# A state-space scan whose decay factors move from SBUF to PSUM, with one 128-channel block and two states per step

## Chip, cores and metric

The kernel runs on one core of one Trainium2 chip. The metric is the device time of one execution in microseconds (us). The kernel before takes 4627.35 us (median of three runs, 4623.8 to 4629.94).

## What is computed

The reference runs one layer of a hybrid model on an input of 8 batches, each of 512 tokens and 256 channels: an attention part with 16 heads, a feed-forward net (FFN) whose operands are quantised to a four-bit format, a two-way Mamba block, and the same FFN again. The change touches the Mamba block. Cut to what matters, it does this once per direction:

```python
x_dbl = xc @ xproj_w                                   # xc: [batch, token, 512 channels]
dt, B_ssm, C_ssm = split(x_dbl, [64, 64 + 16])         # 16 states
dt = softplus(dt @ dt_w + dt_b)
dA = exp(dt[..., None] * A)                            # [.., channel, state]
dBu = dt[..., None] * B_ssm[:, :, None, :] * xc[..., None]
h = dA_t * h + dBu_t                                   # over the tokens
y_t = sum over states of h * C_t
y = y + xc * D_skip
```

There are 8 batches x 2 directions x 512 channels x 16 states of such recurrences, each 512 tokens long.

## The kernel before, in words

The work is written as Python generators. `thread_a` is attention of a batch, `thread_b` the FFNs, the merge and the front of Mamba (`mamba_pre`), and `thread_s` the scan (`ssm`) with its preparation (`ssm_prep`). `interleave` takes rounds of them in turn. A scheduler that knows the dependences then orders each engine's instructions, once, when the kernel is built. On the chip each engine runs its own list strictly in that order, so an instruction that waits also holds everything behind it on its engine. DMAs are issued by SyncE (SP), which has such a list too.

The scan (`ssm`, L818) holds 128 channels on the partitions and 512 tokens along the free dimension. A step handles **two blocks of 128 channels in one state**. There are 8 x 2 x 2 x 16 = 512 steps, each with these instructions:

- L825: SP loads the B row and the C row of the state, repeated on all 128 partitions (tile `rep`, 512 KB, four buffers). Its source `bcd` is a scratch tensor in memory.
- L829: ScalarE computes two exponentials 128x512 into `abuf` in SBUF, the decay factors. There is one such buffer (`NA = 1`).
- L830: VectorE multiplies `u` (step size times input) by B into `hbuf`, 128x1024. There are three `hbuf` buffers.
- L834: VectorE runs one `tensor_tensor_scan` over both blocks, 128x1026. A zero column between the blocks stops the recurrence. Direction 1 runs over reversed views.
- L835: GpSimd multiplies `hbuf` by C in place, 128x1024. The text below calls it the step's product with C.
- L838: TensorE adds the eight 128x128 pieces into PSUM by transposing matmuls. One bank per block sums all 16 states (`y0`, `y1`).

After 16 steps ScalarE copies the sums out (L844), TensorE transposes them back (L127), VectorE adds `xc * D_skip` (L852), and SP writes the result (L853).

The eight PSUM banks are shared out by name: `pa` 2 and `po` 1 for attention, `pb` 2 for FFN and merge, `pp` 1 for Mamba's front, the scan's preparation and its transposes back, `y0` and `y1` for the sums.

Other lines that the prediction names: L384, L438 and L443 (attention, VectorE reading PSUM), L573 and L574 (FFN, VectorE reading PSUM and SBUF), L755 (merge, VectorE reading PSUM and SBUF), L500 to L510 (quantisation: VectorE, with GpSimd at L506 and L510), L693 and L695 (convolution of Mamba's front, VectorE with two SBUF inputs), L270 to L275 (reciprocal square root, tiny VectorE instructions), L811 to L816 (preparation of the scan, GpSimd and VectorE), L469 (attention, ScalarE's exponentials from PSUM to SBUF).

Of the kernel before, what the change touches and what calls it, by code (L numbers as in the profile page):

```python
# [18 lines left out]
P = 128  # L19
# [16 lines left out]
def shape_constants():  # L36
    """Tables and masks that depend on shapes alone, side by side in one array."""
    inv = (1.0 / (np.float32(10000.0) ** (np.arange(0, LAT, 2, dtype=np.float32) / np.float32(LAT)))).astype(np.float32)
    fr = np.outer(np.arange(T, dtype=np.float32), inv).astype(np.float32)
    cos = np.repeat(np.cos(fr), 2, axis=-1).astype(np.float32)  # L40
    sin = np.repeat(np.sin(fr), 2, axis=-1).astype(np.float32)
    cos = np.tile(cos.T, (4, 1))
    sin = np.tile(sin.T, (4, 1))
    p = np.arange(P)
    mask8 = (p[:, None] // HD == np.arange(8)[None, :]).astype(np.float32)
    mask4 = (p[:, None] // LAT == np.arange(4)[None, :]).astype(np.float32)
    up = np.where(p[None, :] > p[:, None], NEG, 0.0).astype(np.float32)
# [15 lines left out]
def tile_hybrid(ctx: ExitStack, tc: tile.TileContext, w: dict, consts: bass.AP, out: bass.AP):  # L63
# [11 lines left out]
    PB, TB, HB, QB, QA, HT = 2, 3, 3, 3, 2, 1  # L75
    LAG, TC, XB, YT = 2, 4, 3, 2
    NH4, NA, NU, NDT, TA, RB = 3, 1, 3, 2, 2, 4
# [8 lines left out]
    BANKS = {"pa": 2, "po": 1, "pb": 2, "pp": 1, "y0": 1, "y1": 1}  # L86
# [13 lines left out]
    # ---------------------------------------------------------------- constants  # L100
# [52 lines left out]
    def prep_attention():  # L153
# [6 lines left out]
        q2r = work([P, LAT], F32, "qmx", 4)  # L160
        k2r = work([P, LAT], F32, "qns", 4)
        l2r = work([LAT, HD], F32, "l2r", 1)
        wqr = work([P, LAT], F32, "qrs", 4)
# [11 lines left out]
        k2n = work([LAT, HD], F32, "k2n", 1)  # L175
# [66 lines left out]
        # cproj, transposed, and the vector that every bias behind the softmax adds up to  # L242
# [65 lines left out]
    def token_transpose(dst, src, tag="pb"):  # L308
        """src [P, NT, C] tokens on partitions -> dst [P, 2, T] channels on partitions."""
# [64 lines left out]
    def roped(xT, g, q):  # L374
        """Rotated latents of four heads [latent, token]; q: 0 for queries, 1 for keys."""
# [13 lines left out]
    def spill(hl, order):  # L389
        """hl [(head, latent), high/low, token] -> memory [part, latent, head, token] with the parts in order."""  # L390
# [6 lines left out]
    def latents(xT, g):  # L397
        """High and low parts of the keys and of the queries of four heads, in memory."""
# [27 lines left out]
            # row maxima, negated  # L426
# [62 lines left out]
    # -------------------------------------------------------------------- FFN  # L489
    def fp4(dst, src, n, tag, twice=False, pp=P):  # L490
        """Block-wise FP4 quantise and dequantise of src [pp, n] along the free dim into dst. A multiple of the step
        (half of the power of two below the value, at least 0.5) is what is left when 1.5 * 2**23 steps have been added
        and taken away again; or-ing 22 << 23 into an exponent of 128 or 129 adds 22 to it, and leaves a smaller one
        below 149."""
        nb = n // 16
        mx = work([P, FF // 16], F32, "qmx", 4)[:pp, :nb]
        s3 = src.rearrange("p (b k) -> p b k", k=16)
        V.tensor_reduce(mx, s3, AX.X, ALU.max, apply_absolute_value=True)
        ns = work([P, FF // 16], F32, "qns", 4)[:pp, :nb]
        V.tensor_scalar(ns, mx, -1.0 / 6.0, -2e-12 if twice else -1e-12, ALU.mult, ALU.min)  # L500
        rs = work([P, FF // 16], F32, "qrs", 4)[:pp, :nb]
# [46 lines left out]
    def ffn_front(src):  # L548
        """The normalised and quantised rows, transposed."""
# [52 lines left out]
    def ffns(jobs):  # L602
        """One FFN after the other, as one stream of row tiles; the rows of the next are made ready meanwhile."""
# [26 lines left out]
    # ------------------------------------------------------------------ Mamba  # L630
# [9 lines left out]
    abuf = [const([P, 2, T + 1], F32, f"abuf{i}") for i in range(NA)]  # L640
    hbuf = [const([P, 2, T + 1], F32, f"hbuf{i}") for i in range(NH4)]
    for t in abuf + hbuf:
        G.memset(t, 0.0)
# [53 lines left out]
    def mamba_pre(src, scr):  # L697
# [13 lines left out]
        token_transpose(xT, xn, "pp")  # L711
        yield
        for m in range(8):
            wp = work([P, 2, P], F32, "xrf", XB)
            nc.sync.dma_start(wp, win_d[m])
            o = psum("pp")
# [56 lines left out]
    def ssm_prep(b, d, c, scr):  # L773
        """Step sizes of half the channels in one direction and their products with the input; B and C in memory."""
        sx = ("", "_b")[d]
        if c == 0:
# [6 lines left out]
            o = psum("pp")  # L783
# [17 lines left out]
        for e in range(2):  # L801
            o = psum("pp")
# [15 lines left out]

    def ssm(b, d, scr):
        for c in range(2):  # L820
            dt, u, bcd = prep.pop((b, d, c))
            yps = [psum(f"y{i}") for i in range(2)]
            for n in range(NS):
                bcr = work([P, 2, T], F32, "rep", RB)
                nc.sync.dma_start(bcr, bcd[n][None].to_broadcast([P, 2, T]))  # L825
                seq[0] += 1
                a, h = abuf[seq[0] % NA], hbuf[seq[0] % NH4]
                for m in range(2):
                    S.activation(a[:, m, 1:], dt[:, m, :], AF.Exp, scale=Aneg[:, d, 2 * c + m, n : n + 1])  # L829
                V.tensor_tensor(h[:, :, 1:], u, bcr[:, 0, None, :].to_broadcast([P, 2, T]), ALU.mult)  # L830
                aflat, hflat = a.rearrange("p m t -> p (m t)"), h.rearrange("p m t -> p (m t)")
                if d == 1:
                    aflat, hflat = aflat[:, ::-1], hflat[:, ::-1]
                V.tensor_tensor_scan(hflat, aflat, hflat, 0.0, ALU.mult, ALU.add)  # L834
                G.tensor_tensor(h[:, :, 1:], h[:, :, 1:], bcr[:, 1, None, :].to_broadcast([P, 2, T]), ALU.mult)  # L835
                for m in range(2):
                    for i in range(NT):
                        PE.matmul(yps[m][:, i * P : (i + 1) * P], h[:, m, 1 + i * P : 1 + (i + 1) * P], ident,  # L838
                                  start=(n == 0 and i == 0), stop=(n == NS - 1 and i == NT - 1), is_transpose=True)
                yield  # L840
            yts = []
            for i in range(2):
                yts.append(work([P, T], F32, "yt", YT))
                S.copy(yts[i], yps[i])  # L844
            for i in range(2):
                o = psum("pp")
                for q in range(NT):
                    transpose(o[:, q * P : (q + 1) * P], yts[i][:, q * P : (q + 1) * P])
                xp = work([P, T], F32, "xp", 1)
                m = 2 * c + i  # L850
                nc.sync.dma_start(xp, scr["xc"][4 * d + m])
                V.scalar_tensor_tensor(xp, xp, Dh[:, d, m : m + 1], o, ALU.mult, ALU.add)  # L852
                nc.sync.dma_start(scr["y"][4 * d + m], xp)  # L853
# [13 lines left out]
    def both(*gens):  # L867
        """The generators in turns until every one has ended."""
# [10 lines left out]
    def thread_b(done, pre, new):  # L879
        """Merge and second FFN of batch done, Mamba's front of batch pre, first FFN of batch new."""  # L880
# [4 lines left out]
    def interleave(*gens):  # L885
        """Rounds of the generators, each stretched over the same number of rounds and ahead of its place by a number
        of instructions."""
# [43 lines left out]
    seq = [0]  # L931
# [56 lines left out]
```

## Time and profile before

| what | value |
|---|---|
| median of three runs | 4627.35 us |
| span of the profiled execution | 4625.4 us |
| busy VectorE (DVE) | 4028.7 us |
| busy TensorE (PE) | 3244.4 us |
| busy GpSimd (POOL) | 2201.7 us |
| busy ScalarE (ACT) | 1592.1 us |
| memory moved | 628.44 MB, mean 136 GB/s |
| of it loads of `rep` | 512 of 512 KB |
| first and last scan start | 541.1 and 4502.8 us |

A profile is one execution. Its page gives busy times per engine, the span cut in 40 slices, and the costliest groups of instructions. A group's line names the source line, the engine, the operation, output and inputs with shapes, the count, the busy time and the mean duration in ns of one, and after the last bar how long the engine sat idle before these instructions and on what. Views of the trace add to this: one line's instructions with their shortest, median and longest duration, all instructions of an engine in order of time, busy times per stretch, and who waited for whom. A duration runs from an instruction's start on its engine to its end, so time in which it stands still inside the engine counts as busy.

### The profile page before, as it was taken

To read this page: it belongs to the slowest core of one execution; us is meant where nothing else is said; L and a number is where in the kernel's file an instruction comes from. 1 tells how busy PE (TensorE), PEld (TensorE's weight loads), DVE (VectorE), ACT (ScalarE), POOL (GpSimd) and SP (SyncE) were. 2 spreads that over 40 slices of the span, in tenths; PEclk is the share of its full clock that TensorE was granted. 3 is DMA by queue.
4 is the path that set the end of the run, shared out by engine and by line. 5 is a ranking of instruction groups with operands and counts; after the bars stand their busy time and mean duration, and the time that the engine had idled before them with its cause. 6 is when DMAs were issued, how large, how long until landed. Compare 5 with 4: busy or idle time off the path is not lost. (4 is left out here: it accounts for less than half of the span.)

```text
span 4625.4 us, 40263 instructions
## 1 busy us (share of the span) xinstructions
PE 3244.4 (70%) x12904; PEld 2000.0 (43%) x12904; DVE 4028.7 (87%) x4087; ACT 1592.1 (34%) x2725; POOL 2201.7 (48%) x929
## 2 busy tenths in 40 slices
PE   4879777787776678777777777768745566466456
PEld 2334344344444345444544444445533344345344
DVE  5235599897999996999989998999999999999983
ACT  1223432543443333333343333433433324332320
POOL 3011365445445653545444564565455554555551
PEclk8779878888887799888888888878866777677678
DMA  5223433444454344543454344533543244425232
GB/s 138 85 82 103 141 133 115 152 145 147 159 188 138 115 130 156 166 148 121 153 180 156 119 139 159 185 114 119 167 140 125 100 130 162 147 100 189 98 103 88
DMA packets 349922, 628.44 MB, mean 136 GB/s; under 512 B 50029, under 2 KB 195726, under 8 KB 349710
## 3 DMA queue, kind: packets, MB, share of 16 engines
q1 hardware_dynamic: 349710, 625.85, 41.9%
q8 instruction: 103, 1.69, 0.2%
q14 instruction: 109, 0.89, 0.1%
HBM read 506.85 MB, written 118.88 MB: 135 GB/s over the span
## 5 line engine op out<-in xcount | busy, mean ns | idle before, releaser
L835 POOL TENSOR_TENSOR hbuf<-hbuf,rep 128x1024 f32<-128x1024 f32 x512 | 1304.8, 2549 | 1505.4 <-DVE hbuf L834 688.3
L834 DVE TENSOR_TENSOR_SCAN hbuf<-abuf,hbuf 128x1026 f32<-128x1026 f32 x512 | 1357.7, 2652 | 32.8 <-ACT abuf L829 30.7
L829 ACT ACTIVATE abuf<-dt,Aneg 128x512 f32<-128x512 f32 x1024 | 684.9, 716 | 1699.9 <-DVE hbuf L834 1688.0
L830 DVE TENSOR_TENSOR hbuf<-u,rep 128x1024 f32<-128x1024 f32 x512 | 911.6, 1786 | 37.0 <-issue 19.6
L838 PE MATMUL y<-cst,hbuf 128*128 128x128 f32 x4096 | 690.5, 322 | 355.2 <-POOL hbuf L835 346.7
L838 PEld LDWEIGHTS y<-cst,hbuf 128*128 128x128 f32 x4096 | 579.1, 169 | 517.8 <-POOL hbuf L835 422.9
L98 PE MATMUL pb<-wgu,fxT 128*128 128x352 f32 x1024 | 427.9, 555 | 167.8 <-DVE hff L573 55.5
L433 PE MATMUL pa<-kst,qst 96*128 96x512 f32 (+3 forms) x512 | 229.9, 497 | 237.3 <-DVE tmp L384 100.9
L474 PE MATMUL po<-pt,vs 128*32 128x512 f32 (+3 forms) x1024 | 343.5, 481 | 4.3 <-ACT pt L469 4.2
L98 PEld LDWEIGHTS pb<-wgu,fxT 128*128 128x128 f32 x1024 | 211.5, 223 | 311.3 <-DVE hff L573 75.8
L98 PE MATMUL pa<-xT,wp 128*128 128x512 f32 x512 | 288.1, 694 | 50.4 <-DVE mx L443 29.3
L386 POOL TENSOR_TENSOR tmp<-tmp,tmp 128x512 f32<-128x512 f32 x64 | 124.4, 1944 | 405.8 <-DVE tmp L384 247.6
L98 PE MATMUL pb<-qv,hff 128*128 128x256 f32 x1024 | 261.4, 402 | 38.5 <-DMA qv<-sy 36.0
L98 PE MATMUL pb<-wdn,hT 128*128 128x256 f32 (+1 forms) x768 | 238.9, 455 | 34.5 <-ACT hT L588 14.6
L469 ACT ACTIVATE pt<-pa 128x512 f32<-128x512 f32 x320 | 186.0, 591 | 197.4 <-PE pa L466 135.5
L433 PEld LDWEIGHTS pa<-kst,qst 96*128 96x128 f32 x512 | 120.0, 235 | 305.3 <-DVE tmp L384 123.6
L443 DVE TENSOR_REDUCE mx<-pa 128x1 f32<-128x512 f32 (+2 forms) x384 | 179.0, 497 | 82.7 <-PE pa L435 82.4
L693 DVE SCALAR_TENSOR_TENSOR tmpB<-xs,cw,tmpB 128x512 f32<-128x512 f32 x192 | 243.0, 1265 | 7.6 <-ACT tmpB L691 6.1
L464 PE MATMUL pa<-qst,kst 98*128 98x512 f32 (+3 forms) x512 | 213.5, 464 | 50.4 <-ACT pt L469 23.3
L98 PEld LDWEIGHTS pb<-qv,hff 128*128 128x128 f32 x1024 | 197.3, 201 | 86.0 <-DMA hff<-in_merge_w 22.9
L98 PEld LDWEIGHTS pb<-wdn,hT 128*128 128x128 f32 (+1 forms) x768 | 161.1, 225 | 93.2 <-issue 25.8
L510 POOL TENSOR_TENSOR hff<-qv,qns 128x704 f32<-128x704 f32 x66 | 143.7, 2177 | 104.7 <-DVE qv L509 79.0
(207 smaller groups left out, 4899.3 us busy)
## 6 DMA issues: line engine op xcount, KB each, us to landing
rep<-bcd SPq DMA_DIRECT2D x512, 512.0 KB
hld<-hl SPq DMA_DIRECT2D x192, 256.0 KB
hff<-in_merge_w SPq DMA_DIRECT2D x128, 256.0 KB
qv<-sy SPq DMA_DIRECT2D x128, 256.0 KB
kst<-hld SPq DMA_DIRECT2D x64, 384.0 KB
qst<-hld SPq DMA_DIRECT2D x64, 384.0 KB
wp<-wqk_d SPq DMA_DIRECT2D x64, 256.0 KB
sxc<-tmpB SPq DMA_DIRECT2D x64, 256.0 KB
```

The costliest lines, as they stand in the source:

```text
L98: PE.matmul(o, L, R, start=start, stop=stop, **kw)
L433: PE.matmul(o[:, at : at + n], qst[pr][:96, j, i * P : (i + 1) * P], kst[:96, j, :n], start=(k == 0), stop=False)
L443: V.tensor_reduce(M[:, j, i : i + 1], o[:, at : at + n], AX.X, ALU.max, negate=True)
L464: PE.matmul(o[:, at : at + n], kst[:, j, kt * P : (kt + 1) * P], qst[pr][:, j, kt * P :], start=(k == 0), stop=False)
L469: S.activation(pt, o, AF.Exp)
L474: PE.matmul(po[c : c + 32, kt * P :], vs[:, kt, h * VW : h * VW + 32], pt[:, at : at + n], start=(kt == 0), stop=(kt == 2), tile_position= ...
L693: V.scalar_tensor_tensor(acc, tap(k), cw[:, d, m, k : k + 1], acc, ALU.mult, ALU.add)
L829: S.activation(a[:, m, 1:], dt[:, m, :], AF.Exp, scale=Aneg[:, d, 2 * c + m, n : n + 1])
L830: V.tensor_tensor(h[:, :, 1:], u, bcr[:, 0, None, :].to_broadcast([P, 2, T]), ALU.mult)
L834: V.tensor_tensor_scan(hflat, aflat, hflat, 0.0, ALU.mult, ALU.add)
L835: G.tensor_tensor(h[:, :, 1:], h[:, :, 1:], bcr[:, 1, None, :].to_broadcast([P, 2, T]), ALU.mult)
L838: PE.matmul(yps[m][:, i * P : (i + 1) * P], h[:, m, 1 + i * P : 1 + (i + 1) * P], ident, start=(n == 0 and i == 0), stop=(n == NS - 1 and ...
```

## The change

A step now handles **one block of 128 channels in two states**. There are again 512 steps.

- The decay factors go to PSUM: two banks `a`, one exponential 128x512 each, instead of `abuf` in SBUF. The zero column is gone.
- The scan becomes two instructions of 128x512 per step, each with its factors in PSUM and its `h` in SBUF. `h` has four buffers.
- The B and C rows of two states are loaded together: 1 MB per step instead of 512 KB, and three buffers instead of four. A row that served two blocks is now loaded for each block.
- ScalarE issues these loads, and those of `xp`, instead of SP. Each is queued behind the second exponential of a step, and fetches for two steps later.
- A block's sums take one bank `y`, and are finished after 8 steps; L844 to L853 of before run once per block.
- The banks `pp`, `y0`, `y1` become `a` (2) and `y` (1). What used `pp` now uses `pb`.
- To make room in SBUF the buffers of `qv`, `tmpB`, `yt` and the three small quantisation tiles go down by one each.

The diff, cut to this (some lines with names of pools and tags are left out):

```diff
-    PB, TB, HB, QB, QA, HT = 2, 3, 3, 3, 2, 1
-    LAG, TC, XB, YT = 2, 4, 3, 2
-    NH4, NA, NU, NDT, TA, RB = 3, 1, 3, 2, 2, 4
+    PB, TB, HB, QB, QA, HT = 2, 3, 3, 2, 2, 1
+    LAG, TC, XB = 2, 3, 3
+    NHB, NU, NDT, TA, RB, YT = 4, 3, 2, 2, 3, 1
...
-    BANKS = {"pa": 2, "po": 1, "pb": 2, "pp": 1, "y0": 1, "y1": 1}
+    BANKS = {"pa": 2, "po": 1, "pb": 2, "a": 2, "y": 1}
...
+    def load_rep(b, d, m, n):
+        rep = work([P, 2, 2, T], F32, "rep", RB)
+        src = fronts[(b, d)][1][2 * n : 2 * n + 2].rearrange("n k t -> (n k t)")
+        S.dma_start(rep.rearrange("p n k t -> p (n k t)"), src[None].to_broadcast([P, 4 * T]))
+        return rep
...
-                nc.sync.dma_start(bcr, bcd[n][None].to_broadcast([P, 2, T]))
-                seq[0] += 1
-                a, h = abuf[seq[0] % NA], hbuf[seq[0] % NH4]
-                for m in range(2):
-                    S.activation(a[:, m, 1:], dt[:, m, :], AF.Exp, scale=Aneg[:, d, 2 * c + m, n : n + 1])
-                V.tensor_tensor(h[:, :, 1:], u, bcr[:, 0, None, :].to_broadcast([P, 2, T]), ALU.mult)
...
-                V.tensor_tensor_scan(hflat, aflat, hflat, 0.0, ALU.mult, ALU.add)
-                G.tensor_tensor(h[:, :, 1:], h[:, :, 1:], bcr[:, 1, None, :].to_broadcast([P, 2, T]), ALU.mult)
...
+            y = psum("y")
+            for n in range(NS // 2):
+                rep = reps.pop(0)
+                h = work([P, 2, T], F32, "h", NHB)
+                V.tensor_tensor(h, u[:, m % 2, None, :].to_broadcast([P, 2, T]), rep[:, :, 0, :], ALU.mult)
+                for e in range(2):
+                    a = psum("a")
+                    ex = S.activation(a, dt[:, m % 2, :], AF.Exp, scale=Aneg[:, d, m, 2 * n + e : 2 * n + e + 1])
+                    if d == 0:
+                        V.tensor_tensor_scan(h[:, e], a, h[:, e], 0.0, ALU.mult, ALU.add)
+                    else:
+                        V.tensor_tensor_scan(h[:, e, ::-1], a[:, ::-1], h[:, e, ::-1], 0.0, ALU.mult, ALU.add)
+                with tc.issue_after(ex.ins):
+                    if todo_rep:
+                        reps.append(load_rep(*todo_rep.pop(0)))
+                    if n == 2:
+                        xp = work([P, T], F32, "xp", 1)
+                        S.dma_start(xp, scr["xc"][4 * d + m])
+                G.tensor_tensor(h, h, rep[:, :, 1, :], ALU.mult)
...
-                nc.sync.dma_start(xp, scr["xc"][4 * d + m])
...
```

`tc.issue_after(x)` makes what is written in its block stand behind `x` in its engine's list; it adds no wait for `x` to finish.

More of the change, by code (lines that the diff above doesn't have):

```diff
@@ L159, in prep_attention @@
         nc.sync.dma_start(cab, w["c_attn_b"].rearrange("(a p) -> p a", p=P), allow_slow_non_contiguous=True)
[L160 to L163, printed above, removed]
+        q2r = work([P, LAT], F32, "qmx", 3)
+        k2r = work([P, LAT], F32, "qns", 3)
+        l2r = work([LAT, HD], F32, "rd", 2)
+        wqr = work([P, LAT], F32, "qrs", 3)
         lbr = work([P, 1], F32, "lbr", 1)
@@ L174, in prep_attention @@
         nc.sync.dma_start(l2r, w["l2o_w"].rearrange("d l -> l d"), allow_slow_non_contiguous=True)
-        k2n = work([LAT, HD], F32, "k2n", 1)
+        k2n = work([LAT, HD], F32, "rd", 2)
         nc.sync.dma_start(k2n, w["kv2l_w"])
@@ L495, in fp4 @@
         nb = n // 16
-        mx = work([P, FF // 16], F32, "qmx", 4)[:pp, :nb]
+        mx = work([P, FF // 16], F32, "qmx", 3)[:pp, :nb]
         s3 = src.rearrange("p (b k) -> p b k", k=16)
         V.tensor_reduce(mx, s3, AX.X, ALU.max, apply_absolute_value=True)
-        ns = work([P, FF // 16], F32, "qns", 4)[:pp, :nb]
+        ns = work([P, FF // 16], F32, "qns", 3)[:pp, :nb]
         V.tensor_scalar(ns, mx, -1.0 / 6.0, -2e-12 if twice else -1e-12, ALU.mult, ALU.min)
-        rs = work([P, FF // 16], F32, "qrs", 4)[:pp, :nb]
+        rs = work([P, FF // 16], F32, "qrs", 3)[:pp, :nb]
         V.reciprocal(rs, ns)
@@ L639, in tile_hybrid @@
     TH = T // 2
[L640 to L643, printed above, removed]
     xsb = [const([P, 3 + T + 3], F32, f"xs{i}") for i in range(2)]
@@ L710, in mamba_pre @@
         xT = work([P, 2, T], F32, "fxT", 2)
-        token_transpose(xT, xn, "pp")
+        token_transpose(xT, xn)
         yield
@@ L715, in mamba_pre @@
             nc.sync.dma_start(wp, win_d[m])
-            o = psum("pp")
+            o = psum()
             for ct in range(2):
@@ L782, in ssm_prep @@
             nc.sync.dma_start(wxp, wxp_d[d])
-            o = psum("pp")
+            o = psum()
             for m in range(ND):
@@ L801, in ssm_prep @@
         for e in range(2):
-            o = psum("pp")
+            o = psum()
             PE.matmul(o, wdt[:, e * P : (e + 1) * P], dbt[: DTR + 1, :], start=True, stop=True)
@@ L817, in ssm_prep @@
         yield
-    def ssm(b, d, scr):
[L820 to L824, printed above, removed]
-                nc.sync.dma_start(bcr, bcd[n][None].to_broadcast([P, 2, T]))
-                seq[0] += 1
-                a, h = abuf[seq[0] % NA], hbuf[seq[0] % NH4]
-                for m in range(2):
[L829 to L836, printed above, removed]
+    def load_rep(b, d, m, n):
[3 more added lines that the diff above has]
+        return rep
@@ new lines, in tile_hybrid @@
+    todo_rep = [(b, d, m, n) for b in range(B) for d in range(2) for m in range(ND) for n in range(NS // 2)]
+    reps = []
+    def ssm(b, d, scr):
+        for m in range(ND):
+            if m % 2 == 0:
+                dt, u, _ = prep.pop((b, d, m // 2))
+            while len(reps) < 2:
+                reps.append(load_rep(*todo_rep.pop(0)))
[13 more added lines that the diff above has]
+                    if todo_rep:
+                        reps.append(load_rep(*todo_rep.pop(0)))
+                    if n == 2:
+                        xp = work([P, T], F32, "xp", 1)
+                        S.dma_start(xp, scr["xc"][4 * d + m])
+                G.tensor_tensor(h, h, rep[:, :, 1, :], ALU.mult)
+                for e in range(2):
@@ L837, in ssm @@
                     for i in range(NT):
-                        PE.matmul(yps[m][:, i * P : (i + 1) * P], h[:, m, 1 + i * P : 1 + (i + 1) * P], ident,
-                                  start=(n == 0 and i == 0), stop=(n == NS - 1 and i == NT - 1), is_transpose=True)
+                        PE.matmul(y[:, i * P : (i + 1) * P], h[:, e, i * P : (i + 1) * P], ident,
+                                  start=(n == 0 and e == 0 and i == 0), stop=(n == NS // 2 - 1 and e == 1 and i == NT - 1), is_transpose=True)
@@ L840, in ssm @@
                 yield
[L841 to L850, printed above, removed]
-                nc.sync.dma_start(xp, scr["xc"][4 * d + m])
-                V.scalar_tensor_tensor(xp, xp, Dh[:, d, m : m + 1], o, ALU.mult, ALU.add)
-                nc.sync.dma_start(scr["y"][4 * d + m], xp)
+            yt = work([P, T], F32, "yt", YT)
@@ L855, in scratch @@
+            S.copy(yt, y)
+            o = psum()
+            for q in range(NT):
+                transpose(o[:, q * P : (q + 1) * P], yt[:, q * P : (q + 1) * P])
+            V.scalar_tensor_tensor(xp, xp, Dh[:, d, m : m + 1], o, ALU.mult, ALU.add)
+            nc.sync.dma_start(scr["y"][4 * d + m], xp)
     def scratch(b):
@@ L930, in tile_hybrid @@
     fronts = {}
-    seq = [0]
     prep_attention()
```

## The prediction, made before the changed kernel was run

> **What bounds the kernel now.** I read the page's busy times and slices first, then the costliest groups, then single lines with their shortest, median and longest durations, then two short stretches in order of time.
>
> ```profile
> span 4625.4 us, 40263 instructions
> PE 3244.4 (70%) x12904; PEld 2000.0 (43%) x12904; DVE 4028.7 (87%) x4087; ACT 1592.1 (34%) x2725; POOL 2201.7 (48%) x929
> DVE  5235599897999996999989998999999999999983
> ```
>
> VectorE is the bound: nearly full in every slice from the fifth to the last but one. In the stretch with scans (580 to 4510 us) it is busy 3711.5 of 3930 us, so only 218 us of idle time can be taken up there. But how much of this "busy" is work?
>
> ```profile
> L835 POOL TENSOR_TENSOR hbuf<-hbuf,rep 128x1024 f32<-128x1024 f32 x512 | 1304.8, 2549 | 1505.4 <-DVE hbuf L834 688.3
> L834 DVE TENSOR_TENSOR_SCAN hbuf<-abuf,hbuf 128x1026 f32<-128x1026 f32 x512 | 1357.7, 2652 | 32.8 <-ACT abuf L829 30.7
> L830 DVE TENSOR_TENSOR hbuf<-u,rep 128x1024 f32<-128x1024 f32 x512 | 911.6, 1786 | 37.0 <-issue 19.6
> ```
>
> ```profile
> L830 DVE TENSOR_TENSOR hbuf<-u,rep x512: 1154/1220/3378, 537.7 to 4493.5; 128x1024 f32<-128x1024 f32 x171
> L834 DVE TENSOR_TENSOR_SCAN hbuf<-abuf,hbuf x512: 2224/2283/4449, 541.1 to 4502.8; 128x1026 f32<-128x1026 f32 x171
> L503 DVE TENSOR_SCALAR qrs<-qrs x106: 111/174/2251, 65.8 to 4611.5; 128x44 f32<-128x44 f32 x66, 128x32 f32<-128x32 f32 x32, 88x32 f32<-88x32 f32 x8
> L573 DVE SCALAR_TENSOR_TENSOR hff<-hff,pb x128: 453/506/522, 344.3 to 4608.5; 128x352 f32<-128x352 f32 x128
> L755 DVE TENSOR_TENSOR tmpB<-pb,tmpB x32: 657/678/692, 1240.3 to 4555.4; 128x512 f32<-128x512 f32 x32
> ```
>
> Shortest, median, longest in ns. The first three have long tails: a 0.17 us instruction can take 2.25 us. The last two, with one operand in PSUM, have none. The order of time shows why (start, duration in us; VectorE's rows, then GpSimd's):
>
> ```profile
> 2641.67 0.49 DVE L573 SCALAR_TENSOR_TENSOR hff<-hff,pb 128x352 f32<-128x352 f32 x1
> 2642.08 3.06 DVE L830 TENSOR_TENSOR hbuf<-u,rep 128x1024 f32<-128x1024 f32 x1
> ```
>
> ```profile
> 2641.88 2.18 POOL L835 TENSOR_TENSOR hbuf<-hbuf,rep 128x1024 f32<-128x1024 f32 x1 [2.29 <-DVE hbuf L834]
> ```
>
> GpSimd's product runs from 2641.88 to 2644.06. L573, reading PSUM, runs beside it undisturbed. L830, with two SBUF inputs, takes 3.06 us instead of 1.22: it ends at 2645.14, one undisturbed duration after GpSimd. So VectorE instructions with SBUF inputs and GpSimd's exclude each other, and PSUM readers are exempt. I took each VectorE instruction's excess over the median of its own shape where GpSimd was quiet, and the GpSimd instruction that ended just as it got going. The excess sums to 1070 us: 190 us on scans (check: 512 x (2652 - 2283) ns = 189) and 880 us on others (L830: 512 x (1786 - 1220) ns = 290). The step's product with C causes 721 of it, in 480 of 512 cases, because it becomes ready 0.13 us after the scan ends and so meets whatever comes after the scan.
>
> **What the change does to this, part by part.**
>
> 1. *Scans leave the exclusion.* An operation with one SBUF and one PSUM input (L573, L755) never waits, whatever GpSimd does. No scan from PSUM is in the trace; I take it to behave like these. The 190 us on scans go. No other stall stands behind them, since the next VectorE instruction just starts earlier.
>
> 2. *GpSimd can now work under scans.* What of the other 880 us goes? The product with C still becomes ready when the second scan has ended, so most of it still meets what follows. In the built program's VectorE list, the second scan is directly followed by the next step's product with B in 128 of 512 steps. Then GpSimd waits out 1.2 us and runs under the next scans, where before it stopped a scan. Walking down the two lists with the undisturbed durations, the 0.13 us and this exclusion, products with C alone, I count 685 us in 471 collisions before (the trace has 721 in 480, so the walk may be trusted), and 470 in 314 after. Ratio 0.69: 721 becomes 495, less 226 (99 of these on scans). The other GpSimd lines cause 349 us, 92 on scans; I let only these 92 go. Sum: less 318, of which 190 from item 1 and 128 here. Ends: 0 beyond the scans; or all but a third of the 1070, if GpSimd's work slides wholly under the scans (less 700).
>
> 3. *Two scans for one.* L573 (352 elements, 506 ns) and the quiet L830 (1024, 1220) give 1.06 ns per element and 133 fixed. So the scan's own rate is (2283 - 133) / 1026 = 2.10 ns, and one of 512 is 1206 ns: 2412 per pair, 129 more than 2283. Consecutive instructions start some 75 ns before the previous one ends (rows above: 2641.67 + 0.49 against 2642.08), so 54 ns of this stay: 512 x 54 = 28 us. [...] The rows differ: 512 elements with PSUM take 678 ns (L755), without (L695, median) 684. [...] I follow the rows, but lean a little, as no scan is among them: 40.
>
> 4. *Exponentials to PSUM.* No row writes PSUM from ScalarE; L829 (SBUF to SBUF) takes 716 ns, L469 (PSUM to SBUF, same function) 597. Between these, at most 1024 x 0.12 us less on an engine at 34%: nothing. They are as well hidden as now: two banks let the first exponential of a step start when the previous step's first scan is done, and the scan waited for `abuf` 30.7 us in all.
>
> 5. *Loads.* Twice 268 MB for `rep`: 628 becomes 897 MB. Over 4450 us that is 201 GB/s, and some 225 in the stretch with scans; the best slice before had 189, and the busiest of 10 us about 300. A load of 512 KB takes 3.4 us from issue to its last packet (median, 2.5 of it moving), so 1 MB some 6 us alone. It is issued two steps (14 us) ahead, once GpSimd has released the buffer of the step before: about 8 to 10 us of cover. Mostly hidden, and a few steps will be late. Moving the load to ScalarE's queue: the issue cost 327 ns on SP, so 512 + 64 of them are 0.19 ms of an engine that has room. Queued behind each are the next exponentials and the copies from PSUM for attention and FFN. In 370 of 512 cases the load stands ahead of every later exponential, and it waits for GpSimd's product, some 2 us after its own exponential could run. Bounds of this on VectorE: below nothing (SP waited 1334 us on GpSimd at L825, and what stood behind came late; VectorE waited for DMAs some 110 us, of which half may go), and up to 400 (rival B). I take 50, near L834's and L830's present idle times (33 and 37).
>
> 6. *Banks and buffers.* `pb` serves also `pp`'s users, one `y` instead of two, fewer `qv` and `tmpB`. VectorE now waits 82 us for L443's scores and some 90 for `pb` results (L755 34, L573 28, L598 25); a third more of the latter plus the sums' copy: 30, between 0 and 120. SP, TensorE and GpSimd lose nothing on the path, TensorE being busy 2735 of 3930 us in the stretch; at 3650 this would be 75%.
>
> Sum on the profiled span: 4625 - 190 - 128 + 40 + 0 + 50 + 30 = 4427. Runs lie 2 us above the span: about **4430 us**, 4.3% faster. Its own range, with items 2, 5 and 6 at milder ends, is 4320 to 4560.
>
> **Rivals.**
>
> *A: full slide.* GpSimd needs about 1740 us without waiting; after the change scans give 512 x 2.3 = 1180 us of cover, PSUM readers some 850, idle time the rest. If two thirds of the 1070 go: 4625 - 700 + 40 + 80 = about 4045; halfway, where I put it, 4200. For it: the cover is there. Against: the data dependence that puts each product just behind the scans, and 430 of 512 steps have the next product with B after the scan, too.
>
> *B: slower, the ring of three B/C buffers.* A buffer is filled, read by VectorE, scanned, read by GpSimd, and only then may ScalarE issue its next load. Its round: product with B, scans and what stands between, 6 us; GpSimd 2.3 to 3.4; ScalarE's queue 1 to 2; the load 6. That is about 16 us for three steps, 5.3 each, against VectorE's 7 per step ((3930 - 300) / 512). From a load of about 11 us on (traffic at 225 GB/s, bursts from SP's queue) the ring decides: at 14 us it is 25.4 / 3 = 8.5 us per step, 512 x 1.4 = 720 more than 4430. At 12 us, 7.8 and some 4830, which I take. [...] Against: 10 us stretches of 300 GB/s.
>
> *C: a scan keeps the exclusion with PSUM too,* so the change doesn't do what it says: 4625 + 40 + 80 = 4745 or less. L573, L574 and L755 speak against it.
>
> **How the numbers follow.** Chances: forecast 0.52, A 0.18, B 0.22, C 0.08. Faster by over 0.2% (9 us, about what a measurement of this kernel can tell from no change): the forecast's and A's, less 0.02 of the forecast's upper tail, 0.68. Within 0.2%: that 0.02 and 0.03 of mild forms of B and C, 0.05. Slower: the rest of B and C, 0.27. The range for 8 in 10 reaches from A to C, 4200 to 4750; it leaves out half of A and half of B.
>
> **What would show it.** Item 1: the scans' longest duration close to their median, near 1.2 us. If it has a tail to 3 us, C. Item 2: L830's successor with a mean of about 1.6 us instead of 1.79, the product with C still often right behind the scans. [...] Item 5: VectorE idle before its product with B, on a DMA, under 60 us; hundreds mean B. I am wrong if VectorE is no longer 90% busy in the stretch with scans.

## The result and the profile after

The changed kernel takes **4640.8 us** (median of six runs, 4632.9 to 4655.7) against 4627.3 us before (six runs, 4623.8 to 4630.5). The ratio is **1.0029**, with a 95% interval of 1.0015 to 1.0042. It is 0.3% slower, where 4.3% faster was forecast. The time lies inside the range of 4200 to 4750, on the wrong side of the kernel before. The profiled execution took 4632.94 us.

First the head of the page after:

```profile
span 4631.1 us, 41283 instructions
...
PE 3238.4 (70%) x12904; PEld 2009.0 (43%) x12904; DVE 3764.2 (81%) x4599; ACT 1620.6 (35%) x2725; POOL 2066.1 (45%) x925
...
DVE  5335589899699888997888897999899979898873
```

VectorE does 265 us less (4028.7 to 3764.2), close to the 278 that the prediction's first three items make. Yet the span has not moved, so its idle time has grown from 597 to 867 us, by 270. Many slices that showed a 9 before show a 7 or an 8.

Did the change do what it says? Three lines of the trace after, with shortest, median and longest duration in ns (L842 and L844 are the scans of the two directions, L837 is the product with B):

```profile
L842 DVE TENSOR_TENSOR_SCAN h<-a,h x512: 1148/1203/1225, 548.4 to 4287.4; 128x512 f32<-128x512 f32 x171
L844 DVE TENSOR_TENSOR_SCAN h<-a,h x512: 1154/1205/1225, 803.2 to 4499.5; 128x512 f32<-128x512 f32 x171
L837 DVE TENSOR_TENSOR h<-u,rep x512: 1148/1219/3407, 546.2 to 4497.0; 128x1024 f32<-128x1024 f32 x171
```

The scans have lost their tail: the longest takes 1225 ns, where one of 2283 could take 4449 before. The product with B, with two SBUF inputs, keeps its own. In order of time, VectorE's rows and then GpSimd's:

```profile
3515.56 2.34 DVE L844 TENSOR_TENSOR_SCAN h<-a,h 128x512 f32<-128x512 f32 x2
3517.81 1.20 DVE L837 TENSOR_TENSOR h<-u,rep 128x1024 f32<-128x1024 f32 x1
3519.11 2.34 DVE L844 TENSOR_TENSOR_SCAN h<-a,h 128x512 f32<-128x512 f32 x2
3521.37 0.49 DVE L573 SCALAR_TENSOR_TENSOR hff<-hff,pb 128x352 f32<-128x352 f32 x1
```

```profile
3518.12 3.09 POOL L851 TENSOR_TENSOR h<-h,rep 128x1024 f32<-128x1024 f32 x1 [3.76 <-DVE h L844]
```

This is the picture that item 2 drew. GpSimd's product with C starts at 3518.12, stands still until VectorE's product with B ends at 3519.01, and then runs 2.2 us under two scans. These take 2.34 us together, as the two before them do. The groups in the page say how often it goes otherwise:

```profile
L851 POOL TENSOR_TENSOR h<-h,rep 128x1024 f32<-128x1024 f32 x512 | 1376.0, 2688 | 1537.1 <-DVE h L842 448.6
L840 ACT ACTIVATE a<-dt,Aneg 128x512 f32<-128x512 f32 x1024 | 701.8, 690 | 1489.2 <-DVE h L844 758.5
L837 DVE TENSOR_TENSOR h<-u,rep 128x1024 f32<-128x1024 f32 x512 | 889.3, 1740 | 85.7 <-DMA rep<-bcd 43.8
```

L837 still averages 1740 ns against a median of 1219, so it is often stopped; item 2 had named about 1.6 us as its sign. Worked out as in the prediction, VectorE's excess fell from 1070 to 750 us. The part caused by the step's product with C fell from 721 us (480 collisions) to 604 (358).

So where did 270 us of idle time come from? The longest waits of VectorE before, and then after:

```profile
DVE mx L443 <- PE pa L435: 82.4, 26, 20.2
...
DVE hff L573 <- ACT hff L572: 27.6, 13, 5.9
DVE tmp L384 <- PE pa L98: 25.9, 19, 3.0
DVE xrf L598 <- PE pb L98: 25.4, 11, 9.6
...
DVE xp L852 <- PE pp L127: 6.9, 2, 5.3
```

```profile
DVE mx L443 <- PE pa L435: 104.5, 36, 20.3
DVE hff L573 <- ACT hff L572: 81.2, 34, 6.8
DVE xrf L598 <- PE pb L98: 64.5, 19, 11.4
DVE tmp L384 <- PE pa L98: 47.6, 32, 4.1
...
DVE h L837 <- DMA rep<-bcd: 43.8, 33, 5.1
DVE h L837 <- PE y L854: 34.8, 15, 5.8
...
DVE xp L862 <- PE pb L127: 32.4, 16, 10.9
```

The columns are us in total, times, longest; L862 was L852 before. The new waits stand at users of `pb` first (L573 and L598, 93 us more), and hardly any at the scan itself. By engine, gaps ended by TensorE grew from 283 to 419 us, by ScalarE from 123 to 203, by GpSimd from 20 to 64, by DMAs from 136 to 150.

### The profile page after: what moved, and what is told of

Its sections match the earlier page's. It is cut to its first block, busy times and chain, and to the rows that moved or that the text cites. A ratio compares the mean times of both kernels' runs of the same rounds, so it can differ in the third digit from the quotient of the medians.

```text
span 4631.1 us, 41283 instructions
## 1 busy us (share of the span) xinstructions
PE 3238.4 (70%) x12904; PEld 2009.0 (43%) x12904; DVE 3764.2 (81%) x4599; ACT 1620.6 (35%) x2725; POOL 2066.1 (45%) x925
## 4 chain that ended last, share of the span: by engine, by line
DVE 49%; PE 13%; issue 10%; DMA 10%; POOL 3%; ACT 3%; SPq 0%; ACTq 0%; DVEq 0%; POOLq 0%
DVE h L837 13%; DVE h L844 9%; DVE h L842 8%; PE pb L98 7%; DMA rep<-bcd 4%; POOL h L851 2%; DVE tmpB L689 2%; PE po L474 2%; DVE qv L508 2%; DVE mx L443 2%; PE y L854 1%; PE pa L98 1%; DVE qa L507 1%; DMA tmpB<-ssz 1%; DVE qmx L498 1%
## 5 line engine op out<-in xcount | busy, mean ns | idle before, releaser
L851 POOL TENSOR_TENSOR h<-h,rep 128x1024 f32<-128x1024 f32 x512 | 1376.0, 2688 | 1537.1 <-DVE h L842 448.6
L840 ACT ACTIVATE a<-dt,Aneg 128x512 f32<-128x512 f32 x1024 | 701.8, 690 | 1489.2 <-DVE h L844 758.5
L837 DVE TENSOR_TENSOR h<-u,rep 128x1024 f32<-128x1024 f32 x512 | 889.3, 1740 | 85.7 <-DMA rep<-bcd 43.8
L854 PE MATMUL y<-cst,h 128*128 128x128 f32 x4096 | 663.3, 319 | 368.1 <-POOL h L851 355.6
L854 PEld LDWEIGHTS y<-cst,h 128*128 128x128 f32 x4096 | 567.9, 166 | 493.6 <-POOL h L851 411.8
L844 DVE TENSOR_TENSOR_SCAN h<-a,h 128x512 f32<-128x512 f32 x512 | 598.3, 1204 | 14.0 <-ACT a L840 7.0
L842 DVE TENSOR_TENSOR_SCAN h<-a,h 128x512 f32<-128x512 f32 x512 | 598.2, 1204 | 6.5 <-ACT a L840 1.1
L474 PE MATMUL po<-pt,vs 128*32 128x128 f32 (+3 forms) x1024 | 351.9, 489 | 22.8 <-ACT pt L469 22.7
L386 POOL TENSOR_TENSOR tmp<-tmp,tmp 128x512 f32<-128x512 f32 x64 | 95.4, 1491 | 409.7 <-DVE tmp L384 280.2
L443 DVE TENSOR_REDUCE mx<-pa 128x1 f32<-128x512 f32 (+2 forms) x384 | 179.7, 500 | 105.0 <-PE pa L435 104.5
L689 DVE SCALAR_TENSOR_TENSOR tmpB<-xs,cw,tmpB 128x512 f32<-128x512 f32 x192 | 208.9, 1088 | 20.0 <-ACT tmpB L687 18.1
L98 PE MATMUL pb<-fxT,xrf 128*128 128x512 f32 x256 | 156.1, 742 | 68.2 <-DVE tmpB L751 21.6
```

What stands on the lines that cost most here:

```text
L98: PE.matmul(o, L, R, start=start, stop=stop, **kw)
L443: V.tensor_reduce(M[:, j, i : i + 1], o[:, at : at + n], AX.X, ALU.max, negate=True)
L474: PE.matmul(po[c : c + 32, kt * P :], vs[:, kt, h * VW : h * VW + 32], pt[:, at : at + n], start=(kt == 0), stop=(kt == 2), tile_position= ...
L689: V.scalar_tensor_tensor(acc, tap(k), cw[:, d, m, k : k + 1], acc, ALU.mult, ALU.add)
L837: V.tensor_tensor(h, u[:, m % 2, None, :].to_broadcast([P, 2, T]), rep[:, :, 0, :], ALU.mult)
L840: ex = S.activation(a, dt[:, m % 2, :], AF.Exp, scale=Aneg[:, d, m, 2 * n + e : 2 * n + e + 1])
```

## The experiments

The letters in the expectations: **L**, the doubled traffic of loads costs; **Q**, issuing them from ScalarE's queue costs; **P**, what used `pp` now shares `pb`, and that costs; **B**, the smaller buffers (`qv`, `tmpB`, `yt`, the small quantisation tiles) cost (not the prediction's rival B); **O**, the built order of an engine's list decides; **S**, a chain of the other engines, hidden before, sets the time when VectorE has less to do. "VectorE's list" is its list of instructions as the scheduler built it. Every edit lets the scheduler build the lists anew, so each run holds its edit and the order that comes with it. Ratios are to the kernel before, with 95% intervals.

### Is it the traffic, or the queue?

`a_half_bytes`: the changed kernel loads the rows of one state only.

```diff
-        src = fronts[(b, d)][1][2 * n : 2 * n + 2].rearrange("n k t -> (n k t)")
-        S.dma_start(rep.rearrange("p n k t -> p (n k t)"), src[None].to_broadcast([P, 4 * T]))
+        src = fronts[(b, d)][1][2 * n : 2 * n + 1].rearrange("n k t -> (n k t)")
+        S.dma_start(rep[:, :, 0, :], src.rearrange("(k t) -> k t", k=2)[None].to_broadcast([P, 2, T]))
...
-                G.tensor_tensor(h, h, rep[:, :, 1, :], ALU.mult)
+                G.tensor_tensor(h, h, rep[:, :, 0, :], ALU.mult)
```

> The changed kernel with half the bytes per load: it loads the B and the C row of one state (512 KB instead of 1 MB per step) and uses these two rows in place of the two B rows; the product with C takes the same rows, so B and C of the second state are left out and the output is not the reference's. Number of loads, queue, buffers and all arithmetic instructions stay. Theory P (the shared PSUM banks pb make TensorE's and ScalarE's results late for VectorE): no change, 4620 to 4650 us, VectorE idle 840 us or more. Rival L (the doubled traffic makes transfers late): the lost 250 us come back for the larger part, 4380 to 4500. Rival S (VectorE's lists in fixed order meet a chain of other engines that was hidden before): no change as well.

Measured 4634.7 us, 1.0009 (0.9998 to 1.0020), with VectorE idle 862 us (867 in the changed kernel). The doubled bytes cost 0.2%, about 9 us, and by the two intervals not above 0.4%. L falls.

`a_loads_on_sp`: SP issues the loads of `rep` again.

```diff
-        S.dma_start(rep.rearrange("p n k t -> p (n k t)"), src[None].to_broadcast([P, 4 * T]))
+        nc.sync.dma_start(rep.rearrange("p n k t -> p (n k t)"), src[None].to_broadcast([P, 4 * T]))
```

> The changed kernel with the B and C loads issued by SP, as before the change; xp stays on ScalarE's queue. Rival Q (a load waiting for GpSimd holds ScalarE's exponentials and copies): 4400 to 4550 us, VectorE's idle time on ScalarE's results from 203 back to about 120 us. Theories P, L and S: within 0.7% of 4640, or slower, since SP waits on GpSimd again.

Measured 4567.2 us, 0.9864 (0.9836 to 0.9891): 73 us less than the changed kernel. That is a little above what Q expected, and well outside what its rivals did. So the queue costs time, but not by the road I expected: gaps ended by ScalarE stay (203 and 206 us). Gaps ended by DMAs fall from 150 to 119, by GpSimd from 64 to 50, and VectorE's busy time by 24 (excess 722 instead of 750). The choice of the issuing engine was worth 1.6% of the time here, with 512 issues of 326 ns each (median) on ScalarE's queue.

### What is left without the product with C?

`a_no_c` and `b_no_c` delete GpSimd's product with C (L851 after, L835 before), so the sums are not weighted by C.

> The changed kernel without the product with C on GpSimd (left out, so the output is not the reference's; the sums take h itself). It takes away 604 us of VectorE standing still behind this product and 1376 us of GpSimd. If VectorE is still the bound: 4640 - 604 = about 4050 us, or less. Theories P and S: most of it turns into idle time, 4300 to 4550 us. Rival L: 4350 or more, with VectorE idle on rep rising from 44 us to hundreds.

> The kernel before without the product with C (left out, so the output is not the reference's). It takes away 721 us of VectorE standing still and 1305 us of GpSimd. If VectorE is the bound: 4627 - 721 = 3900 to 4000 us. Rival S (the chain of the other engines lies just below in this kernel too): 4300 or more, and the same time as the changed kernel without the product within 2%. Theory P: the kernel before gains at least 100 us more than the changed one does.

Measured 4216.9 us (0.9115, 0.9088 to 0.9141) and 3992.0 us (0.8621, 0.8600 to 0.8642). The product with C costs the kernel before 635 us and the changed one 424. That is 211 us less, but only 117 of them are fewer collisions with it. A saved stall is also worth less in the changed kernel: without the product, VectorE's idle time grows by 194 us there and by 131 in the kernel before. `b_no_c` came out as expected for a kernel that VectorE bounds, so S falls for the kernel before. `a_no_c` lies between its two expectations.

Without the product, the changed kernel is 225 us slower than the kernel before. So most of what was lost lies not in the collisions with this product, but in what the change does besides.

### Banks and buffers, put alone into the kernel before

`b_shared_pb` takes only the bank `pp` away and leaves one bank empty.

```diff
-    BANKS = {"pa": 2, "po": 1, "pb": 2, "pp": 1, "y0": 1, "y1": 1}
+    BANKS = {"pa": 2, "po": 1, "pb": 2, "y0": 1, "y1": 1}
...
-            o = psum("pp")
+            o = psum()
...
```

> The kernel before with one edit of the change alone: what used the PSUM bank pp uses the two banks pb, and a bank stays empty. All else, the scan included, as before. Theory P (sharing pb makes results late for VectorE): slower by 60 to 200 us, 4690 to 4830, with VectorE idle before the FFN's and the merge's instructions that read pb. Rival S (any list in fixed order, only less covered): within 0.5% of 4630 us. A bound on P: VectorE is fuller here than in the changed kernel, so part of the lateness may stay covered.

`b_small_bufs` takes only the buffers.

```diff
-    PB, TB, HB, QB, QA, HT = 2, 3, 3, 3, 2, 1
-    LAG, TC, XB, YT = 2, 4, 3, 2
+    PB, TB, HB, QB, QA, HT = 2, 3, 3, 2, 2, 1
+    LAG, TC, XB, YT = 2, 3, 3, 1
...
-        mx = work([P, FF // 16], F32, "qmx", 4)[:pp, :nb]
+        mx = work([P, FF // 16], F32, "qmx", 3)[:pp, :nb]
...
```

> The kernel before with another edit of the change alone: one buffer less each for qv, tmpB, yt and the three small quantisation tiles. Theory B (fewer buffers couple the engines): slower by 50 us or more. Theory P: within 0.5% of 4630 us.

Measured 4801.6 us (1.0370, 1.0352 to 1.0387) and 4746.2 us (1.0243, 1.0228 to 1.0258): **170 and 115 us for edits that I had costed at 30 together.** S had expected no change of `b_shared_pb`. VectorE's busy time hardly moves in either (4025.5 and 4011.2 us), so the cost is idle time: 768 and 723 us of it, 597 before. Its waits with `pb` shared:

```profile
DVE xrf L598 <- PE pb L98: 67.3, 23, 8.6
DVE hbuf L834 <- ACT abuf L829: 63.4, 76, 11.4
DVE xp L852 <- DMA xp<-sxc: 62.9, 12, 12.4
DVE hff L573 <- ACT hff L572: 47.1, 24, 5.9
```

And with the smaller buffers:

```profile
DVE tmpB L693 <- ACT tmpB L691: 59.1, 11, 22.6
DVE hbuf L834 <- ACT abuf L829: 51.3, 78, 2.3
...
DVE tmpB L733 <- ACT tmpB L732: 33.9, 14, 4.7
```

L598 waited 25 us before, L852 for its load 16, L693 6, L733 12.5, the scan 31. With the bank shared, VectorE waits 61 us more for FFN's results (L598, L573), which use `pb`. It also waits 47 us more for the load of `xp` (L852) and 33 us more at the scan. I read the wait for `xp` as a chain (the transposes back come late, so `xp` comes free late, so its next load is late); no run isolates it.

One rival stays untested. The clock that TensorE was granted goes along with the time: 0.80 before, 0.79 with `pb` shared, 0.85 in `b_no_c`. No run holds it fixed. TensorE is busy 36 us longer with `pb` shared than before, so by that estimate a slower clock can be a part of the 170 us, but not most of it.

### Do these costs exist in the changed kernel?

`a_sp_bufs`: SP issues the loads, the rows of one state only are loaded (512 KB, both states use the same B and C), and the room that this leaves restores the small buffers.

> The changed kernel with SP issuing the loads, and with the buffers of qv, tmpB, yt and the three small tiles as before the change. The room comes from loading one state's two rows per step (512 KB; B and C of the second state are left out, so the output is not the reference's), which by the run with half the bytes changes the time by nothing. Theory B: 4450 to 4520 us against 4567 with SP alone. Theory P: 4540 to 4590, VectorE's idle time still near 790 us.

Measured 4512.9 us, 0.9743 (0.9727 to 0.9759): 54 us below `a_loads_on_sp`, and half bytes alone gave about 9. B holds here too, at half its size in the kernel before or less.

`a_sp_pp_in_po` moves the former users of `pp`, but for the first transposes of Mamba's front, to attention's bank `po` instead of `pb`.

> The changed kernel with SP issuing the loads, and with what used the bank pp before (Mamba's front, the scan's preparation, the transposes back) moved from pb to po, the bank of attention's outputs, which is empty once attention is done (after about 3300 us). Theory P, in the changed kernel too: 4440 to 4530 us against 4567 with SP alone, the FFN's waits of VectorE on pb results (L598, L573, L574: 72, 68 and 25 us) down by half; or the gain shows in the stretch after 3300 us alone, where attention can't lose by it. If sharing a bank costs the same wherever it is: 4550 to 4620.

Measured 4735.2 us, 1.0230 (1.0214 to 1.0245), a miss. L598's wait does fall from 72 to 15 us, but L443's grows from 89 to 152 and L485's from 41 to 92. The contention moves to attention, and costs more there.

`x1_pp_in_pb` and `x2_own_pp` need a free bank. They take it from the decay factors, with one constant bank instead of the exponentials (these are left out). SP issues the loads in both. They differ only in where `pp`'s users sit; the first leaves a bank empty.

```diff
-    BANKS = {"pa": 2, "po": 1, "pb": 2, "a": 1, "y": 1}
+    BANKS = {"pa": 2, "po": 1, "pb": 2, "a": 1, "y": 1, "pp": 1}
...
-            o = psum()
+            o = psum("pp")
...
```

> The changed kernel with its loads issued by SP and without the exponentials: one constant bank a serves as decay factors for all scans (the real decay factors are left out), the former users of pp sit on pb as in the changed kernel, and one PSUM bank stays empty. It is the base for x2_own_pp. Theory P (sharing pb costs VectorE waits) expects nothing of it alone: about 4400 to 4570 us, at or below the 4567 of the version with exponentials, as ScalarE has 1024 fewer instructions of 0.69 us.

> As x1_pp_in_pb (the real decay factors left out in the same way), but the former users of pp have the empty bank for themselves. Theory P expects it 60 to 200 us faster than x1_pp_in_pb (the same sharing cost the kernel before 170), with less VectorE idle at L573, L598 and L862. If the changed kernel's idle time is made by other things (order, ScalarE), it is within 25 us of x1_pp_in_pb.

Measured 4567.9 us (0.9862, 0.9844 to 0.9880) and 4492.7 us (0.9695, 0.9679 to 0.9711). The first equals `a_loads_on_sp` (4567.2): 1024 exponentials on ScalarE cost nothing that shows, as item 4 said. The second is 75 us less. Waits of the two:

```profile
DVE xrf L598 <- PE pb L98: 64.9, 20, 14.3
DVE hff L573 <- ACT hff L572: 62.8, 32, 6.1
...
DVE h L840 <- PE y L854: 38.3, 17, 7.9
```

```profile
DVE hff L573 <- ACT hff L572: 32.1, 14, 6.0
...
DVE xrf L598 <- PE pb L98: 20.5, 10, 4.9
...
DVE xp L862 <- PE pp L127: 15.0, 8, 6.5
```

P holds in the changed kernel, at 75 us instead of 170. The two lines that the shared bank should hurt lose 75 us of waiting between them. (L840 is the product with B here; its wait for `y` is gone in the second, though `y` has one bank in both.)

`x3_two_y`: as `x1_pp_in_pb`, with the free bank as a second `y` (`"y": 2`).

> As x1_pp_in_pb (one constant bank of decay factors, the real ones left out), but the empty bank becomes a second bank y for the sums. In the changed kernel VectorE waits 35 us at its product with B (L837) and 25 us more than before at L862 for TensorE's sums in the one bank y. Theory Y (one bank of sums costs these waits) expects 30 to 70 us less than the 4568 of x1_pp_in_pb. If these waits only move on, it is within 15 us.

Measured 4570.2 us, 0.9872 (0.9851 to 0.9893). Against 4567.9 that is nothing. The wait of the product with B for `y` falls from 38 to 21 us, but others take it over. A miss for theory Y.

`x4_all_undone`: as `x2_own_pp`, with the small buffers restored and 512 KB per step.

> As x2_own_pp (real decay factors left out), with the small buffers of the kernel before restored too; for room the B and C rows of one state only are loaded, 512 KB per step, so both states use the same B and C. If the costs add (sharing pb 75, small buffers 54, measured apart), it takes 4567 - 75 - 54 = 4440 us, within 25. If they overlap or the scheduler's order decides, 4460 to 4500. If the prediction's first terms alone remain (4627 - 190 - 128 + 40 = 4349), 4350 to 4400.

Measured 4473.3 us, 0.9662 (0.9646 to 0.9678): 19 us below `x2_own_pp` instead of 54, so the costs overlap. And 124 us above the 4349 of the prediction's first three items are left. They show in two places: VectorE's idle time is 660 us (597 before), and its excess is 814 (750 in the changed kernel).

```profile
span 4465.4 us, 39875 instructions
PE 3185.3 (71%) x12904; PEld 1988.7 (45%) x12904; DVE 3805.0 (85%) x4599; ACT 950.0 (21%) x1702; POOL 2111.3 (47%) x925
```

With fewer waits, VectorE meets GpSimd more often again.

### A product with C that comes later

If the product with C meets what follows the scan, let it come later: `a_sp_skew` (SP issues the loads) makes it wait for the next step's product with B, so that it starts when scans start. `finish` issues the product with C, which waits for `tt`, and the sums of the step before.

```diff
...
+                tt = V.tensor_tensor(h, u[:, m % 2, None, :].to_broadcast([P, 2, T]), rep[:, :, 0, :], ALU.mult)
+                if n:
+                    finish(n - 1, prev, y, tt)
...
```

> The changed kernel with SP issuing the loads, and with the product with C of a step made to wait for the next step's product with B (7 of 8 steps), so that it runs under the next two scans. If the collisions that are left (604 us behind the product with C in the changed kernel) come from the product starting right behind the scans: they fall to 200 us or less, L837's mean from 1740 to 1400 ns, and the time by 100 to 300 us to 4270 to 4470. If the lateness of other engines' results is what counts now: VectorE's busy time falls but the idle time takes most of it, 4520 to 4600.

Measured **4394.0 us, 0.9488** (0.9473 to 0.9502).

```profile
L847 DVE TENSOR_TENSOR h<-u,rep 128x1024 f32<-128x1024 f32 x512 | 724.1, 1417 | 248.1 <-DMA rep<-bcd 206.0
```

The product with B (L847 here) averages 1417 ns instead of 1783 in `a_loads_on_sp`, and the collisions with the product with C are down from 571 us there to 247, where 200 or less was expected. But VectorE now waits 206 us for `rep`: each buffer is held one step longer, so the ring of three is late, as the next run bears out. That is the wait of the prediction's rival B, appearing where the product is late.

`skew_split` gives B and C rows a tile each (512 KB, three buffers each), so that B's comes free early. `skew_split_bufs` takes B's down to two and restores `tmpB` and `yt`.

```diff
-        rep = work([P, 2, 2, T], F32, "rep", RB)
+        rb = work([P, 2, T], F32, "rep", 3)
...
+        rc = work([P, 2, T], F32, "repc", 3)
...
```

> The run with the later product with C, and in addition B rows and C rows of a step in two tiles of 512 KB with three buffers each, in place of one of 1 MB with three (the same bytes and the same room in SBUF). A B buffer is then free after VectorE's product and need not wait for GpSimd's. If the 206 us that VectorE stood before its product with B on the load come from the ring of three buffers, which the later product made longer: this wait falls below 60 us and the time to 4200 to 4320. If they come from traffic: no change, 4360 to 4420.

> As the run before, with two B buffers in place of three, and the room given back to tmpB (4) and yt (2) as before the change. Theory B: 40 to 80 us under the run with the split alone. If two B buffers are too few: VectorE waits for the load again, 100 us or more, and the time is that of the later product alone, 4350 to 4420.

Measured 4630.6 us (0.9999, 0.9988 to 1.0011) and 4466.1 us (0.9653, 0.9632 to 0.9673). The wait for `rep` in `skew_split` is gone (4 us), with the same bytes, so it was the ring. But the gain is gone too, which neither expectation had: collisions with the product with C are back at 467 us. The cause is in VectorE's list. In this build the scheduler put the product with B ahead of the *previous* step's second scan in 353 of 512 steps (27 in `a_sp_skew`), so waiting for it no longer delayed anything. `skew_split_bufs` has 249 such steps, and lies 165 us below, where 40 to 80 were expected; buffers and order are mixed in it.

`skew_split_pin` and `skew_split_bufs_pin` keep the product with B behind that scan by an order edge without a wait (0 of 512 ahead).

> As skew_split, but the product with B is kept behind the previous step's second scan in VectorE's list by an order edge without a wait. Theory O (the built order took away the later product's gain, the tiles did not): collisions of the product with C fall from 467 to 250 us or less, VectorE waits for loads below 60 us (206 in a_sp_skew), time 4200 to 4320 us. Rival: the ring of buffers or GpSimd sets the pace in some other way; then the time stays between 4390 and 4630 us.

> As skew_split_pin with four tmpB and two yt again, and two buffers for the B rows instead of three. Theory B (fewer small buffers cost VectorE waits) with theory O expects 40 to 80 us below skew_split_pin, 4150 to 4260 us. If two buffers for B are too few, it is slower than skew_split_pin and VectorE waits over 100 us for the loads of B.

Measured 4416.5 us (0.9533, 0.9519 to 0.9547) and **4327.9 us (0.9338, 0.9316 to 0.9360)**. The product with B in the first:

```profile
L850 DVE TENSOR_TENSOR h<-u,rep 128x1024 f32<-128x1024 f32 x512 | 690.5, 1349 | 48.2 <-PE y L835 37.4
```

The order brings back 214 of the 237 us that `skew_split` had lost; collisions with the product with C are 282 us. So O holds for what `skew_split` had lost. But the time is above the 4200 to 4320 that I expected, inside the rival's range: 206 us of waiting for `rep` are gone against `a_sp_skew`, and the time is no better. Gaps ended by ScalarE grew from 175 to 260 us, by TensorE from 416 to 469, by GpSimd from 54 to 80, and collisions by 41. I read this as the wait at the load having stood in for waits that come anyway. Restoring `tmpB` and `yt`, with two B buffers instead of three, gives 89 us on top, more than the 40 to 80 expected. It makes the fastest kernel here that leaves nothing out: 6.6% below the kernel before, though above the 4150 to 4260 expected.

## Why the prediction was wrong

**Item 1's 190 us and item 3 were right, in mechanism and in size; item 2's sum is luck.** Forecast: excess less 318 (scans 190, others 128); measured less 320, the scans' 190 included. Rival C is dead by the scans' longest duration. Inside item 2 two errors cancel. The product with C lost 117 instead of 226; other GpSimd lines went from 349 to 146 where I had let only 92 go. The total is luck once more: in `x4_all_undone`, without the queue, bank and buffers that slow the changed kernel, the excess falls by 256 only. The walk down the lists knew no waits of other engines; I think that this misled it. Item 3: VectorE's busy time outside the excess grew by 55 us (2958.7 to 3014.1), forecast 40. The scan from PSUM takes 1204 ns, forecast 1206 by the rows. The 40 holds 12 us beyond the 28 of the rows, for scans slower than that; no run shows this term, and what the runs showed is scans that kept to the rows. Item 4 was right (`x1_pp_in_pb`).

**The step that failed is item 6**, "a third more of the latter plus the sums' copy: 30, between 0 and 120". Alone in the kernel before, the bank costs 170 us and the buffers 115. In the changed kernel they cost 75 and 19 to 54, by what is undone first. I scaled the waits that the profile of before showed at `pb`. That is no measure of what a new user of the bank costs: in `b_shared_pb` the waits at L598 and L573 grow from 53 to 114 us, and waits for other things than the bank grow too. I also gave the small buffers no price of their own, since no row of before showed a wait for them.

**A second step failed with it:** item 1's "No other stall stands behind them, since the next VectorE instruction just starts earlier". The sum took each us that VectorE stops losing as a us gained. In `b_no_c`, with banks and buffers untouched, 757 us less busy time brought 131 us more idle time. The forecast is 211 us from the result. By the runs taken in turn, item 6 makes 64 of them (75 + 19 against 30) and ScalarE's queue 23 (73 against 50). The other 124 had no term.

**Item 5 was about right in sum and wrong in reason.** The traffic is nearly free (9 us). ScalarE's queue costs 73 us, forecast 50 for both. (VectorE's wait for DMAs in the kernel before was 136 us, not 110.) The wait of the product with B for its load, 43.8 us, was under the 60 I had set, so rival B had the direction and not the cause. That the range holds 4641 is owed to the end that it has from rival C. The sentence "I am wrong if VectorE is no longer 90% busy in the stretch with scans" came true: 3455.98 of 3930 us, 88%, against 94% before. Before and after:

```profile
580.00:4510.00 3930.00, 2735.38 (x11119) 1727.22 (x11119) 3711.50 (x3415) 1425.56 (x2401) 2067.34 (x834) 0.80 0.43 141
580.00:4510.00 3930.00, 2726.89 (x11139) 1734.56 (x11139) 3455.98 (x3934) 1456.92 (x2406) 1936.88 (x833) 0.80 0.60 208
```

The third time behind the comma (3711.50 and 3455.98) is VectorE's.

The forecast's sum with the measured terms: excess -320, other busy time +55, idle time +270, together +5 on a span of 4625.4; measured 4631.1. Forecast were -318, +40 and +80. Nearly all of the miss is idle time.

**What stays open.** Taken out in turn, queue (73), bank (75) and buffers (19) explain 167 of the 292 us between 4641 and 4349. The other 124 appear as idle time and new collisions once those are undone (63 and 64 us). I think that the scheduler's order makes them, as it did in `skew_split`; no run holds the order of the kernel before fixed, so this is argued, not shown. The order did change: the product with B stands ahead of the step before's last scan in 336 of 512 steps before the change, in 82 after, in 137 in `x4_all_undone`. But `a_half_bytes` has 173 such steps and nearly the time of the changed kernel, so this count alone does not decide. Why the loads on ScalarE's queue cost 73 us, when ScalarE's own waits don't shrink with them, is not settled either.

## What to carry to other kernels

Speeding up the bound engine by taking banks and buffers from its feeders can give it all back (here 265 us less busy time became 270 us more idle time): cost every bank and buffer by a run that takes only it away, since the waits of before show what it costs while it is there. The scans and products with one operand in PSUM ran beside GpSimd undisturbed (the longest scan took 1225 ns with medians of 1203 and 1205, the longest L573 of before 522 with a median of 506), but this pays only as far as GpSimd's work lands beside them, so move the work there and look at the built order. A wait that is removed is a gain only when nothing else is late in its place: 206 us of waiting for loads were worth nothing here.

## What the runs showed of the hardware

- The scans with their factors in PSUM showed nothing of the exclusion with GpSimd: 1024 of them took between 1148 and 1225 ns, where the ones over two blocks from SBUF (before, L834) had a median of 2283 and took up to 4449. Nor did the products with one PSUM operand: 128 at L573 of before took between 453 and 522.
- GpSimd's product seems to depend on how its operands are laid out. With one row read twice (before, L835) its shortest takes 2160 ns; with 1024 different elements (after, L851) 2337, and L811 of before, likewise without repetition, 2339. That is 0.18 us on each of 512. `hbuf` of before also has a column more per block, and no run changes the one without the other.
- ScalarE's exponential takes 690 ns on average to PSUM (L840) and 716 to SBUF (L829), as item 4's bounds had it.
- The runs that leave one of the eight PSUM banks empty were slower: `b_shared_pb` by 170 us against the kernel before, `x1_pp_in_pb` by 75 against `x2_own_pp`. But using all eight is not enough here. `x3_two_y` uses the eighth for a second `y` and takes 4570 us, where `x1_pp_in_pb` takes 4568: it counts who gets the bank.
